# A sequence's group norm moved into the next sequence's first group, and its output projections one group later

## The chip, the cores and the metric

The kernel runs on one core of a Trainium2 chip. A core has TensorE (matmuls; PE in the profile, with PEld for its weight loads), VectorE (DVE), ScalarE (ACT), GpSimd (POOL) and SyncE (SP), whose queue issues most of the transfers. Each engine works through its own list of instructions in order and waits on semaphores for the others. Matmuls write to PSUM, which has eight banks here. The metric is the device time of the core in microseconds; lower is better.

## What is computed

x has 8 sequences of 512 tokens with 512 features. After a layer norm, the block computes a linear attention with decay in 16 heads, multiplies its output by a sigmoid gate, normalises each head's 32 features by their root mean square, and projects with Wo. Beside it stands a mixture of 16 experts (4 for each token) with a shared expert. The result is x + s * silu(ffn). Cut to what matters here:

```python
x = o * jax.nn.sigmoid(gate)
xg = x.reshape(b, n, HEADS, HEAD_DIM)
ms = jnp.mean(xg * xg, axis=-1, keepdims=True)
xg = xg * jax.lax.rsqrt(ms + EPS)
return xg.reshape(b, n, d) * weight      # then o @ Wo
# the block
x = L0_attn_x
xn = _layernorm(x, axis=-1)
s = _L0_attn_ref(xn, ...)
g = _silu(_L0_ffn_ref(xn, ...))
x = x + s * g
```

## The kernel before, in words

There are three stages. The first norms x, routes the tokens to experts and does the attention of sequences 0 and 1. The second runs the experts block by block. The third, which starts at about 740 us, does the attention of sequences 2 to 7 and, beside it, gathers the experts' results, adds them up and writes the output. Only the third is touched; `carry` is an empty list until it begins, so code under `if carry` belongs to it.

An attention sequence b works on the transposed activations xT: 4 groups g of 4 heads (128 features), 4 chunks of 128 tokens. In `sequence`, each group issues:

- `scores(b, g)` (L673): 12 small state matmuls (L684), then 16 score matmuls into four PSUM banks ps_0 to ps_3 (L695); a scan on VectorE gives the carried state, ScalarE copies it into a block matrix (L704), and VectorE multiplies the four banks by the decay mask into sc (L720).
- `step()`: a little work of the mixture of experts (`advance`, L1274): gathers and additions on GpSimd, two additions on VectorE (L1226, L1230), a Silu on ScalarE (L1233).
- for groups 0 and 1 the key and the query of two groups ahead (`rotated`, L637: a product of four matmuls, Silu on ScalarE, then shuffle, multiply by cos, multiply by sin and an addition on VectorE, L643 to L647); for groups 2 and 3 the value products of the next sequence (L587).
- `by_token` (L656): three transposes of the next group's keys.
- up to two deferred output projections of the sequence before (`project`, L785), by the table `fill`; `projected` is here `finish`, which multiplies the projection into the mixture's tile on VectorE (L1253), whereupon GpSimd adds x (L1257) and SP stores the tile.
- `output(b, g)`: the attention output (L731, L742), multiplied into the gate on VectorE (L746).

After the four groups comes the tail. With `defer`, as in the third stage, it issues the next sequence's gate (`gate_2`, L617, four Sigmoids) and last value product, and the norm of b itself: `squares` (L749: four Squares on ScalarE; 16 matmuls that sum them over each head into one bank, L756; a Sqrt, L760), `inverse` (a reciprocal on VectorE, L764), `normed` (L766: 16 matmuls that spread the factors over the features into four banks pb_0 to pb_3, L773; four multiplies on VectorE, L778). Between these stand the keys and queries of the next sequence's groups 0 and 1. `last_sequence` is the version for sequence 7, which has no next one; it projects sequence 6 from its own group 1 on.

What sets the order: within `on_pe()` and `behind(...)` a block is chained behind the last instruction of its engine; other instructions are put in order by a scheduler, and on each engine that order is then fixed. PSUM banks come from one pool by tag: four banks "a", two "d", one "k", one "m" (L105). An allocation of a tag takes the bank that was allocated longest ago, and the writer waits until that bank's readers are done. Key products and even value products take "m"; query products, odd value products, attention outputs and projections take "d"; scores (ps), gates (p2), the norm's sums (pr) and factors (pb) take "a".

Of the kernel before, what the change touches and what calls it, by code (L numbers as in the profile page):

```python
# [95 lines left out]
def tile_block(ctx: ExitStack, tc: tile.TileContext, a: dict, out: bass.AP):  # L96
# [8 lines left out]
    def bank(tag, name):  # L105
        return pp.tile([P, 512], F32, tag=tag, name=name, bufs={"a": 4, "k": 1, "m": 1, "d": 2}[tag])
# [474 lines left out]
    def value(b, t):  # L581
        if t == 0:
            v_of[b] = att.tile([P, NC, D], F32, tag="v", name=f"v_{b}", bufs=2)
        pv = bank("d" if t % 2 else "m", f"pv_{b}_{t}")
        for k in range(KC):
            with on_pe():
                nc.tensor.matmul(  # L587
                    pv, lhsT=xT_of[b][:, k, t * P : (t + 1) * P], rhs=wv[:, k, :],
                    start=(k == 0), stop=(k == KC - 1))
            between[0]()  # L590
        nc.scalar.copy(v_of[b][:, t, :], pv)
# [16 lines left out]
    def gate_2(b, tiles=range(NC)):  # L608
        if 0 in tiles:
            on_of[b] = home(b).tile([P, G, N], F32, tag="on", name=f"on_{b}", bufs=1)  # L610
        g1 = g1_of[b]
        p2s = {t: bank("a", f"p2_{b}_{t}") for t in tiles}
        with on_pe():
            for g in range(G):
                for t in tiles:
                    tq = slice(t * Q, (t + 1) * Q)
                    nc.tensor.matmul(  # L617
                        p2s[t][:, g * P : (g + 1) * P], lhsT=wg2[tq, g * P : (g + 1) * P],
                        rhs=g1[tq, :], start=True, stop=True)
        for t in tiles:  # L620
            nc.scalar.activation(
                on_of[b][:, :, t * P : (t + 1) * P],
                p2s[t].rearrange("p (g n) -> p g n", n=P), AF.Sigmoid)
        if NC - 1 in tiles:
            g1_of.pop(b)
# [27 lines left out]
    def query(b, g):  # L653
        qT_of[g] = rotated(b, g, "q", wq)
# [92 lines left out]


    def squares(b):  # L749
        pr = bank("a", f"pr_{b}")  # L750
        for g in range(G):
            sq = scr[0].tile([P, N], F32, tag="sc", name=f"sq_{b}_{g}", bufs=4)
            nc.scalar.activation(sq, on_of[b][:, g, :], AF.Square)
            with on_pe():
                for c in range(NC):
                    nc.tensor.matmul(  # L756
                        pr[c * Q : (c + 1) * Q, :C], lhsT=sel[:, H - HG - g * HG :][:, :Q],
                        rhs=sq[:, c * C : (c + 1) * C], start=(g == 0), stop=(g == G - 1))
        rs = att.tile([P, C], F32, tag="tmp", name=f"rs_{b}", bufs=TMP)
        nc.scalar.activation(rs, pr[:, :C], AF.Sqrt, bias=eps_rms, scale=1.0)  # L760
        rs_of[b] = rs

# [39 lines left out]
    def sequence(b, step, projected, before=None, defer=False, also=lambda: None):  # L802


        n = b + 1

        def project_tiles(q, ts):
            if q is not None:
                for t in ts:
                    projected(q, t, project(q, t))  # L810


        fill = ([0], [1], [2], [3], [], [], [], [])
        for g in range(G):
            scores(b, g)
            step()
            if g + 2 < G:
                key(b, g + 2)
            else:
                value(n, 2 * (g - 2))  # L820
            if g + 1 < G:
                by_token(b, g + 1)
            project_tiles(before, fill[2 * g])
            step()
            if g + 2 < G:
                query(b, g + 2)
                if g + 3 == G and n not in xT_of:
                    load_xT(n)
            if g + 2 == G:
                value(n, 1)  # L830
            if g == 0 and b not in on_of:
                gate_2(b)
            project_tiles(before, fill[2 * g + 1])
            if fill[2 * g + 1] == [NC - 1]:
                on_of.pop(before, None)
            output(b, g)
            if defer and g + 2 == G:
                gate_1(n)
            step()
        v_of.pop(b)  # L840
        if n == FIRST:
            gate_1(n)
            squares(b)
            inverse(b)
            value(n, 3)
            normed(b)
            return
        if defer:
            gate_2(n)
        value(n, 3)  # L850
        also()
        squares(b)
        step()
        inverse(b)
        key(n, 0)
        also()
        query(n, 0)
        normed(b)
        also()
        if not defer:  # L860
            step()
        key(n, 1)
        by_token(n, 0)
        if defer:
            step()
        query(n, 1)
        also()
        if not defer:
            gate_1(n)
            project_tiles(b, [0, 1])  # L870
            also()
            project_tiles(b, [2, 3])
            also()
            on_of.pop(b)
        step()

    def last_sequence(b, step, projected, before):


        pbs_of, sums = {}, []  # L880

        def squares_of(g):
            sq = scr[0].tile([P, N], F32, tag="sq", name=f"sq_{b}_{g}", bufs=2)
            nc.scalar.activation(sq, on_of[b][:, g, :], AF.Square)
            pr = bank("k" if g + 1 == G else "a", f"pr_{b}_{g}")
            with on_pe():
                for c in range(NC):
                    nc.tensor.matmul(
                        pr[c * Q : (c + 1) * Q, :C], lhsT=sel[:, H - HG - g * HG :][:, :Q],
                        rhs=sq[:, c * C : (c + 1) * C], start=True, stop=True)  # L890
            rs = att.tile([P, C], F32, tag="tmp", name=f"rs_{b}_{g}", bufs=TMP)
            nc.scalar.activation(rs, pr[:, :C], AF.Sqrt, bias=eps_rms, scale=1.0)
            nc.vector.reciprocal(rs, rs)
            rs_of[g] = rs

        def normed_of(g):
            rs = rs_of.pop(g)
            pbs = [bank(tag, f"pb_{b}_{g}_{c}")
                   for c, tag in enumerate("mddk" if g + 1 == G else "aaaa")]
            with on_pe():  # L900
                for c in range(NC):
                    cq = slice(c * Q, c * Q + H)
                    nc.tensor.matmul(
                        pbs[c][:, :C], lhsT=wge[cq, g * P : (g + 1) * P], rhs=rs[cq, :],
                        start=True, stop=True)
            for c in range(NC):
                oc = on_of[b][:, g, c * C : (c + 1) * C]
                nc.vector.tensor_tensor(oc, oc, pbs[c][:, :C], ALU.mult)

        def add_up(t, groups):  # L910
            if t == len(sums):
                sums.append(bank("a", f"pw_{b}_{t}"))
            with on_pe():
                for g in groups:
                    nc.tensor.matmul(  # L915
                        sums[t], lhsT=on_of[b][:, g, t * P : (t + 1) * P], rhs=wo[:, g, :],
                        start=(g == 0), stop=(g == G - 1))

        def project_before(t):
            projected(before, t, project(before, t))  # L920

        for g in range(G):
            scores(b, g)
            step()
            if g + 2 < G:
                key(b, g + 2)
            if g > 1:
                project_before(2 * g - 3)
            if g:
                squares_of(g - 1)  # L930
            if g + 1 < G:
                by_token(b, g + 1)
            step()
            if g + 2 < G:
                query(b, g + 2)
            if g in (1, 2):
                project_before(2 * g - 2)
                normed_of(g - 1)
            output(b, g)
            step()  # L940
        kept.clear()
        add_up(0, (0, 1))
        normed_of(G - 2)
        add_up(1, (0, 1))
        squares_of(G - 1)
        step()
        add_up(2, (0, 1))
        add_up(0, (2,))
        add_up(1, (2,))
        normed_of(G - 1)  # L950
        step()

        add_up(3, (0,))
        add_up(0, (3,))
        projected(b, 0, sums[0])
        add_up(3, (1,))
        add_up(1, (3,))
        projected(b, 1, sums[1])
        add_up(2, (2,))
        add_up(2, (3,))  # L960
        projected(b, 2, sums[2])
        add_up(3, (2, 3))
        projected(b, 3, sums[3])
        step()
# [399 lines left out]
```

## Time and profile before

| | |
|---|---|
| median of 3 runs | 1169.23 us (1165.0, 1169.23, 1175.48) |
| profiled execution | 1169.4 us, its span 1167.6 us, mean granted clock 0.996 |
| PE busy in the span | 1134.0 us (97%) |
| DVE, ACT, POOL busy | 705.6 us (60%), 460.2 us (39%), 452.2 us (39%) |
| 16 spreading matmuls (L773) of one norm | 1.17 us |
| 16 sum-of-squares matmuls (L756) of one norm | 1.08 us |
| product of four matmuls (L631, L785) | 3.60 us |
| score product (L720), one bank | 677 ns |

How to read it: a row of the timeline gives start, duration, engine, line, operation, what is written and read with the shapes, a count, and in brackets how long the engine stood idle before and what ended that. A line of the waits gives engine, line and tile, what was waited for, the total, the number of times and the longest. Matmuls are pipelined, so a row's duration runs some 0.1 us into the next row, and each matmul of the code shows as two there (a product of four as x8).

### The profile page before, as it was taken

Reading aid. Unit: us, or ns where it says so; the run is one execution under the profiler, and the core shown is the slowest. Engines: PE = TensorE matmul, PEld = TensorE weight load, DVE = VectorE, ACT = ScalarE, POOL = GpSimd, SP = SyncE. Lnnn points to the kernel's source line nnn. Section 1 sums busy time; section 2 is a strip of 40 time slices with the busy share of each in tenths; the row PEclk is TensorE's granted clock in tenths of the full one; section 3 lists DMA queues with packets and bytes.
Section 4 is the critical chain, followed back from the end, with each engine's and each line's share of the span. In section 5 each row is a group of like instructions: output and inputs, shape, how many; then the busy total and the mean of one; then the engine's idle time right before and its main releaser. Section 6 shows DMA issues by size and latency. Waiting matters only on the chain. (4 is left out here: it accounts for less than half of the span.)

```text
span 1167.6 us, 21692 instructions
## 1 busy us (share of the span) xinstructions
PE 1134.0 (97%) x7780; PEld 694.6 (59%) x7780; DVE 705.6 (60%) x1496; ACT 460.2 (39%) x1042; POOL 452.2 (39%) x432
## 2 busy tenths in 40 slices
PE   7999999989999999999999999999999999999997
PEld 3445554455577677777777775555554645545553
DVE  6358735996134344444444443968879598697784
ACT  3323324254364444444444442352252532523541
POOL 3213103200223333333333331782886858858211
PEclk9999999998999999999999999999999999999999
DMA  9975521290769989999999996951846637535012
GB/s 341 330 251 186 179 106 46 101 361 2 232 153 227 219 228 219 229 233 218 230 223 231 230 226 159 359 148 64 277 128 181 215 100 255 154 119 153 28 38 72
DMA packets 163787, 217.45 MB, mean 186 GB/s; under 512 B 89824, under 2 KB 99168, under 8 KB 161760
## 3 DMA queue, kind: packets, MB, share of 16 engines
q1 hardware_dynamic: 142272, 144.14, 41.9%
q0 software_dynamic: 21120, 70.34, 22.3%
q8 instruction: 65, 1.06, 0.4%
q10 hardware_dynamic: 288, 1.57, 0.4%
q14 instruction: 42, 0.34, 0.1%
HBM read 125.73 MB, written 72.43 MB: 170 GB/s over the span
## 5 line engine op out<-in xcount | busy, mean ns | idle before, releaser
L1112 PE MATMUL pgu<-wexp,xt 128*128 x1088 | 257.9, 380 | 2.7 <-ACT xt L1093 2.2
L1112 PEld LDWEIGHTS pgu<-wexp,xt 128*128 128x128 f32 x1088 | 205.8, 190 | 90.4 <-issue 29.5
L1071 POOL DMA_INDIRECT xg<-xn_d,slot x79 | 74.9, 948 | 243.0 <-DVE y L1142 156.4
L1095 ACT COPY xt<-pl 128x512 uint16<-128x512 uint16 x136 | 104.3, 767 | 142.9 <-DMA pl<-xg 75.9
L1117 DVE TENSOR_TENSOR slb<-slb,pgu 128x128 f32<-128x128 f32 x136 | 39.1, 288 | 196.6 <-ACT slb L1116 196.5
L1215 POOL DMA_INDIRECT yg<-y_d,place x128 | 142.4, 1112 | 31.4 <-issue 18.4
L1133 PE MATMUL py<-wexp,hT 128*128 x272 | 139.2, 594 | 0.0
L587 PE MATMUL pv<-wv,xT 128*128 128x512 f32 x256 | 122.2, 614 | 3.8 <-DMA xT<-xT_d 2.8
L631 PE MATMUL pk<-xT,wk 128*128 128x512 f32 x256 | 118.3, 603 | 0.0
L631 PE MATMUL pq<-xT,wq 128*128 128x512 f32 x256 | 115.9, 593 | 0.3 <-PEq L1177 0.3
L785 PE MATMUL pw<-wo,on 128*128 128x512 f32 x224 | 100.6, 596 | 5.5 <-DVE m L1253 4.9
L1071 POOL DMA_INDIRECT more<-xn_d,slot x57 | 53.8, 944 | 108.3 <-DVE y L1142 107.4
L1257 POOL TENSOR_TENSOR xo<-xo,m 128x512 f32<-128x512 f32 x31 | 45.3, 1461 | 128.4 <-DVE m L1253 121.2
L720 DVE TENSOR_TENSOR sc<-ps,dmask 128x512 f32<-128x512 f32 x128 | 79.1, 677 | 0.9 <-PE ps L695 0.8
L631 PEld LDWEIGHTS pq<-xT,wq 128*128 128x128 f32 x256 | 47.2, 191 | 52.8 <-issue 51.3
L587 PEld LDWEIGHTS pv<-wv,xT 128*128 128x128 f32 x256 | 46.6, 195 | 50.3 <-issue 42.8
L631 PEld LDWEIGHTS pk<-xT,wk 128*128 128x128 f32 x256 | 46.2, 190 | 50.0 <-issue 47.6
L1142 DVE TENSOR_SCALAR y<-py,xg 128x512 f32<-128x512 f32 x79 | 59.2, 750 | 27.4 <-PE py L1133 27.2
L785 PEld LDWEIGHTS pw<-wo,on 128*128 128x128 f32 x224 | 41.2, 190 | 54.9 <-issue 45.4
L1116 ACT ACTIVATE slb<-pgu 128x128 f32<-128x128 f32 x136 | 37.8, 278 | 80.0 <-PE pgu L1112 79.7
L704 ACT COPY blocked<-state 32x96 f32<-32x96 f32 x96 | 30.6, 319 | 79.0 <-DVE state L699 78.1
L1142 DVE TENSOR_SCALAR y<-py,more 128x512 f32<-128x512 f32 x57 | 42.7, 750 | 20.0 <-PE py L1133 20.0
(173 smaller groups left out, 1729.9 us busy)
## 6 DMA issues: line engine op xcount, KB each, us to landing
y_d<-y SPq DMA_DIRECT2D x136, 256.0 KB, 2.9
wexp<-in_experts SPq DMA_DIRECT2D x14, 768.0 KB, 7.8
sh_d<-sh SPq DMA_DIRECT2D x32, 256.0 KB, 3.1
m<-sh_d SPq DMA_DIRECT2D x32, 256.0 KB, 4.4
xo<-in_x SPq DMA_DIRECT2D x32, 256.0 KB, 3.8
out<-xo SPq DMA_DIRECT2D x31, 256.0 KB, 2.0
x<-in_x SPq DMA_DIRECT2D x7, 1024.0 KB, 7.6
xT_d<-xT SPq DMA_DIRECT2D x7, 1024.0 KB, 6.5
```

Of the source, the lines that this page charges most:

```text
L587: nc.tensor.matmul(pv, lhsT=xT_of[b][:, k, t * P : (t + 1) * P], rhs=wv[:, k, :], start=(k == 0), stop=(k == KC - 1))
L631: nc.tensor.matmul(ps, lhsT=w[:, k, g * P : (g + 1) * P], rhs=xT_of[b][:, k, :], start=(k == 0), stop=(k == KC - 1))
L720: nc.vector.tensor_tensor(s, pss[j].rearrange("p (c t) -> p c t", t=C), dmask[:, g * HG + j].unsqueeze(1).to_broadcast([P, NC, C]), ALU.mult)
L785: nc.tensor.matmul(pw, lhsT=on_of[b][:, g, t * P : (t + 1) * P], rhs=wo[:, g, :], start=(g == 0), stop=(g == G - 1))
L1071: nc.gpsimd.indirect_dma_start(out=row(i), out_offset=None, in_=xn_d, in_offset=bass.IndirectOffsetOnAxis(ap=slot[:, i : i + 1], axis=0))
L1095: nc.scalar.copy(xt[:, KP:, :].bitcast(U16).rearrange("p k (t h) -> p h k t", h=2), turned(i).rearrange("p (h k) t -> p h k t", h=2))
L1112: nc.tensor.matmul(pg[:, : 2 * F], lhsT=xt[:, k, :], rhs=wflat[:, bass.ds(off + k * 2 * F, 2 * F)], start=(k == 0), stop=(k == KC - 1))
L1117: nc.vector.tensor_tensor(sl, sl, pg[:, F : 2 * F], ALU.mult)
L1133: nc.tensor.matmul(py, lhsT=hT_of.pop(i), rhs=wflat[:, bass.ds(off_of.pop(i) + KC * 2 * F, D)], start=True, stop=True)
L1142: gone.append(nc.vector.tensor_scalar(y, py, row(i).bitcast(F32)[:, bass.ds(at, 1)], None, ALU.mult).ins)
L1215: nc.gpsimd.indirect_dma_start(out=yg, out_offset=None, in_=y_d, in_offset=bass.IndirectOffsetOnAxis(ap=place[:, r, g : g + 1], axis=0))
L1257: nc.gpsimd.tensor_tensor(xo, xo, m, ALU.add)
```

## The change

The norm of a sequence in the third stage leaves the tail and is issued in the next sequence's group 0: the squares and their sums ahead of the scores, the reciprocal behind them, the spreading and the multiplies behind the query of group 2 and ahead of the attention output. The deferred projections, which need it, move from groups 0 and 1 to groups 1 and 2. The sums take a bank of tag "d" and not "a", and their square roots a tile of their own. In sequence 7, `last_sequence` takes the norm of sequence 6 in the same places; its projections stay. Sequences 0 and 1 keep their order.

```diff
@@ -747,7 +747,7 @@
 
 
     def squares(b):
-        pr = bank("a", f"pr_{b}")
+        pr = bank("d" if carry else "a", f"pr_{b}")
         for g in range(G):
             sq = scr[0].tile([P, N], F32, tag="sc", name=f"sq_{b}_{g}", bufs=4)
             nc.scalar.activation(sq, on_of[b][:, g, :], AF.Square)
@@ -756,7 +756,8 @@
                     nc.tensor.matmul(
                         pr[c * Q : (c + 1) * Q, :C], lhsT=sel[:, H - HG - g * HG :][:, :Q],
                         rhs=sq[:, c * C : (c + 1) * C], start=(g == 0), stop=(g == G - 1))
-        rs = att.tile([P, C], F32, tag="tmp", name=f"rs_{b}", bufs=TMP)
+        rs = scr[0].tile([P, C], F32, tag="rs", name=f"rs_{b}") if carry else att.tile(
+            [P, C], F32, tag="tmp", name=f"rs_{b}", bufs=TMP)
         nc.scalar.activation(rs, pr[:, :C], AF.Sqrt, bias=eps_rms, scale=1.0)
         rs_of[b] = rs
 
@@ -810,9 +811,13 @@
                     projected(q, t, project(q, t))
 
 
-        fill = ([0], [1], [2], [3], [], [], [], [])
+        fill = ([], [], [0], [1], [2], [3], [], [])
         for g in range(G):
+            if g == 0 and before is not None:
+                squares(before)
             scores(b, g)
+            if g == 0 and before is not None:
+                inverse(before)
             step()
             if g + 2 < G:
                 key(b, g + 2)
@@ -830,6 +835,8 @@
                 value(n, 1)
             if g == 0 and b not in on_of:
                 gate_2(b)
+            if g == 0 and before is not None:
+                normed(before)
             project_tiles(before, fill[2 * g + 1])
             if fill[2 * g + 1] == [NC - 1]:
                 on_of.pop(before, None)
@@ -847,6 +854,16 @@
             return
         if defer:
             gate_2(n)
+            value(n, 3)
+            step()
+            key(n, 0)
+            query(n, 0)
+            key(n, 1)
+            by_token(n, 0)
+            step()
+            query(n, 1)
+            step()
+            return
         value(n, 3)
         also()
         squares(b)
@@ -857,21 +874,17 @@
         query(n, 0)
         normed(b)
         also()
-        if not defer:
-            step()
+        step()
         key(n, 1)
         by_token(n, 0)
-        if defer:
-            step()
         query(n, 1)
         also()
-        if not defer:
-            gate_1(n)
-            project_tiles(b, [0, 1])
-            also()
-            project_tiles(b, [2, 3])
-            also()
-            on_of.pop(b)
+        gate_1(n)
+        project_tiles(b, [0, 1])
+        also()
+        project_tiles(b, [2, 3])
+        also()
+        on_of.pop(b)
         step()
 
     def last_sequence(b, step, projected, before):
@@ -920,7 +933,11 @@
             projected(before, t, project(before, t))
 
         for g in range(G):
+            if g == 0:
+                squares(before)
             scores(b, g)
+            if g == 0:
+                inverse(before)
             step()
             if g + 2 < G:
                 key(b, g + 2)
@@ -933,6 +950,8 @@
             step()
             if g + 2 < G:
                 query(b, g + 2)
+            if g == 0:
+                normed(before)
             if g in (1, 2):
                 project_before(2 * g - 2)
                 normed_of(g - 1)
```

## The prediction

> **What bounds the kernel now.** I read the split of the span by stage first, then TensorE's list of waits in the last stage, then the timelines of TensorE and VectorE around the place that is edited, and last the granted clock. Only the last stage is touched, so the first rows are the five sequences of it that matter, cut where each reaches the value product of its third group (columns: window and length, then busy us of PE, PEld, DVE, ACT, POOL with instruction counts, granted clock, DMA share, GB/s).
>
> ```profile
> 758.98:832.97 73.99, 73.99 (x646) 40.57 (x645) 58.41 (x94) 28.34 (x63) 44.97 (x38) 1.00 0.46 145
> 832.97:908.79 75.82, 74.53 (x646) 40.41 (x645) 66.11 (x96) 28.66 (x64) 58.81 (x48) 1.00 0.60 181
> 908.79:985.38 76.59, 74.47 (x645) 40.41 (x645) 60.07 (x95) 28.70 (x64) 56.40 (x48) 1.00 0.56 172
> 985.38:1063.06 77.68, 75.55 (x645) 41.36 (x645) 60.78 (x93) 28.81 (x64) 57.11 (x48) 1.00 0.52 158
> ```
>
> The matmul work is the same in the four windows, and in the first TensorE never stops: 73.99 us is the price of a sequence without a stall. The others lose 1.83, 2.60 and 3.69 us, 8.1 in all. That is all the stage can give back by better order, 0.7% of the kernel. TensorE's waits say where most of it is lost:
>
> ```profile
> PE pw L785 <- DVE m L1253: 4.9, 4, 1.9
> ```
>
> The second deferred projection waits for a bank of tag d that VectorE has not emptied. VectorE is behind in the first two groups of a sequence and idle later. Now the place of the edit, sequence 3 (start, duration, instruction):
>
> ```profile
> 797.34 1.17 PE L695 MATMUL ps<-qT,kT 32*128 32x128 f32 x32
> 798.44 3.70 PE L631 MATMUL pk<-xT,wk 128*128 128x512 f32 x8
> 801.98 0.49 PE L663 MATMUL pk<-ident,kT 128*128 128x128 f32 x3
> ...
> 805.74 3.60 PE L631 MATMUL pq<-xT,wq 128*128 128x512 f32 x8
> 809.17 3.60 PE L785 MATMUL pw<-wo,on 128*128 128x512 f32 x8
> 812.61 0.83 PE L731 MATMUL po<-qd,blocked 128*128 128x128 f32 x6
> ...
> 814.57 1.17 PE L695 MATMUL ps<-qT,kT 32*128 32x128 f32 x32
> ```
>
> ```profile
> 783.55 0.95 DVE L764 RECIPROCAL rs<-rs 128x128 f32<-128x128 f32 x1 [5.68 <-ACT rs L760]
> ...
> 791.85 2.48 DVE L778 TENSOR_TENSOR on<-on,pb 128x512 f32<-128x512 f32 x4
> ...
> 801.33 2.48 DVE L720 TENSOR_TENSOR sc<-ps,dmask 128x512 f32<-128x512 f32 x4
> ...
> 810.07 0.72 DVE L643 STREAM_SHUFFLE swq<-sq 128x512 f32<-128x512 f32 x1
> ```
>
> The reader is to see that VectorE begins the masked score products (801.33) 2.9 us after the scores are done (798.44), and that TensorE does not mind: two projections (pw) lie between those scores and the next ones.
>
> **The change part by part.** It moves 16 sum-of-squares matmuls (1.01 us), 16 spreading matmuls (1.10), four Square (2.19 on ScalarE) and a Sqrt, a reciprocal (0.95) and four norm multiplies (2.48) from the tail of a sequence into the next one's group 0, five times, and four projections (3.43 us each) a group later. TensorE's work is unchanged. The instruction order of the two kernels shows that it does so: in the tail no norm is left; pr stands behind pq_1 and ahead of the first scores, pb between pq_2 and po_0, pw_0 and pw_1 in group 1, pw_2 and pw_3 in group 2.
>
> Sums of squares: the four Squares keep their early place on ScalarE, so pr finds its operands; 0. The bank of tag d is freed by the Sqrt long before pq_2 needs it two products later; 0. On DVE the reciprocal now stands in front of the four score products: 0.95 each time, counted below.
>
> Projections: their multiplies (0.6 each) and GpSimd's additions leave group 0 for groups 1 and 2, where pv products give VectorE time. SP's queue has the same transfers; the xo loads go later, and the xT load, issued at 827.8 for a use at 908.8, has 80 us to spare. 0.
>
> The spread is the costly part. Its four pb banks are of tag a, of which there are four, and the next four allocations of that tag are the score banks of group 1. So ps_1 now waits for the four norm multiplies. In VectorE's new order these stand behind the rotation of query 2. A floor follows: pq_2 ends at T; ScalarE's Silu and the handover take 0.73 (809.34 to 810.07); shuffle, cos and sin 1.93; four multiplies and the last addition of the rotation five slots of 0.60: 5.7. TensorE meanwhile has pb 1.10, po 1.66, states 0.30: 3.1. The last score bank opens at 5.7, and some 0.8 of the 1.10 of scores is left then, so scores end at 6.5 in place of 4.2: at least 2.3 us lost per sequence, 12 in five.
>
> If VectorE is behind, it is more. Let L be how late the score products of group 0 start behind their scores, and m the expert-mixture operations that stand before the norm multiplies. VectorE then needs 2.40 + 2.54 (key rotation) + 1.93 + 3.0 = 9.9 us after that start; TensorE reaches the end of ps_1 after 3.54 + 0.33 + 3.43 + 1.10 + 1.66 + 0.30 + 1.10 = 11.5. The wait is L + m + 9.9 + 0.8 - 11.5 = L + m - 0.8. Before, L is 2.9, 4.6, 5.3, 8.0 (against scores without their own wait) and 2.7 us in sequences 3 to 7. The norm's leaving takes 2.4 off, the reciprocal adds 0.95; scores come 1.1 earlier, the tail's rotations about 1.0: 1.35 less where VectorE is never idle (5 and 6; in 4 a multiply by s moves ahead and leaves about 4.3), unchanged in 3 and 7, where it waits for the next Silu instead. With m of 1.3, 1.3, 1.9, 1.3 and 0.6 from the new order (0.6 to 0.7 each), the waits are 3.4, 4.8, 5.1, 7.1 and 2.5: 23 us. That this bank pair can hold TensorE is in the trace: in sequence 6 the scores, 1.17 elsewhere, took 2.69, behind the norm multiplies (1022.74 to 1025.13).
>
> ```profile
> 1023.73 2.69 PE L695 MATMUL ps<-qT,kT 32*128 32x128 f32 x32
> ```
>
> Against it, the 8.1 us of old losses go: pw_0 and pw_1 come after a pause in which VectorE has caught up (from the last norm multiply to the multiply by pw_0 it has 9 to 11 us of work, TensorE 11.5 before pw_1). I take 2 us off for GpSimd's additions to xo, which left group 0: beside them VectorE's two-input operations took 1.1 to 2.1 in place of 0.68. Net 23 - 8 - 2 = +13.
>
> **The clock.** Rows of stage two, where TensorE stopped for 2.77 and for 0.79 us:
>
> ```profile
> 262.00:264.00 2.00, 0.42 (x1) 0.42 (x2) 2.00 (x5) 0.00 (x0) 0.00 (x0) 0.83 0.06 25
> 264.00:266.00 2.00, 2.00 (x3) 0.75 (x3) 2.00 (x4) 0.28 (x1) 0.00 (x0) 0.50 0.00 0
> ...
> 284.00:286.00 2.00, 2.00 (x6) 0.78 (x5) 1.93 (x3) 0.00 (x0) 0.00 (x0) 0.50 0.00 0
> ```
>
> After both, the clock was 0.50 for some 3.4 us, about 1.6 us of lost work each. The Trainium skill, "TensorE: Matmul & The Clock Gate", section "Why this matters for your kernels", tells to leave no idle gap over about 3 us between matmul bursts, since an idle window halves the clock. By that rule three waits (sequences 4 to 6) drop it, +4.8; by the second row, where 0.79 us amid small matmuls was enough, all five, +8, for pb, po, states and scores are small matmuls too. But gaps of 1.1 to 1.9 us between long matmuls in the last stage left it at 1.00. I take the rule: +5.
>
> ScalarE gets one more table load in each group 0 (Sqrt now stands between Silus, 10 loads for 5): 1.28 us by its row, and the next operation starts as it ends (857.91, then 859.20). "ScalarE: Activation LUTs", section "What ACT_TABLE_LOAD costs", adds 1.38 us of drain per switch. By the row the Silu of key 2 ends as VectorE comes to it in sequences 3 and 7, 0; by the page those two would be 1.4 later, +2.8. The row decides, 0.
>
> **Sum.** The profiled execution took 1169.4 us (span 1167.6), the median of the runs is 1169.23, so they are one. 1169.4 + 13 + 5 = 1187.
>
> **Rivals.** (1) VectorE keeps up and every wait is at its floor, with the clock held: 12 - 8.1 = +4, 1173. For it: VectorE is busy 58 to 66 of 76 us. Against: L never falls under 2.7 in five sequences. (2) Faster: the backlog that stops pw is what counts, and moved to group 1 it vanishes, while the new wait is hidden: -8.1, 1161. It needs the norm multiplies to be done within 3.1 us of pq_2's end, which the order of the rotation ahead of them (2.66 with Silu) allows for one bank of four. Its ceiling is 0.7%, so it is no win of over 1%. (3) The clock falls in all five and pw_1 waits again as before (4.9): 1187 + 3 + 5 = 1195, more if GpSimd's additions meet the rotations.
>
> **How the numbers follow.** Runs spread from 1165 to 1175, so 1% (11.7 us) is about what can be told from no change. Forecast 0.62, its own range 1180 to 1192; floor 0.20; faster 0.08; worse 0.10. Holding 8 in 10: 1172 to 1197. Over 1180.9: most of the forecast and the worst case, 0.70; faster by over 1% 0.03; the rest 0.27.
>
> **What would show it.** Right: scores of group 1 at 3 to 8 us in place of 1.17 in each of sequences 3 to 7, waiting for the norm multiplies; the wait of pw for m gone or under 2 us; the clock at 0.5 after some of these pauses; a tail without holes; periods of 77 to 81 us. Wrong: scores at 1.2 to 2, or the pause in front of pr or of pw. The size is wrong if VectorE's lag at the first products is far from 3 to 7 us.

## The result, and the profile after

The changed kernel takes 1205.86 us (median of 4 runs, 1202.78 to 1213.91) against 1172.36 of the kernel before, run beside it: ratio 1.0294, 95% interval 1.0258 to 1.033, slower. The profiled execution took 1202.78 us with a span of 1201.0, which is 33.4 more than the span of before, and its mean granted clock is 0.981 (0.996 before). The direction was forecast, and so was the wait that causes it, but 1187 was 19 us short and the range ended at 1197.

The place of the loss is the one that was named. TensorE's list of waits in the last stage of the changed kernel (what waits, for what; us in total, times, longest):

```profile
PE ps L695 <- DVE on L779: 22.8, 7, 7.9
PE pb L916 <- DVE on L921: 0.4, 1, 0.4
PE pk L663 <- DVE state L699: 0.3, 1, 0.3
```

The 4.9 us of pw are gone, and the scores of group 1 now wait for the norm multiplies (L779 in the changed file). The windows from the value product of one third group to the next, for sequences 3 to 6 (columns as in the prediction):

```profile
829.33:914.05 84.72, 78.60 (x648) 43.84 (x644) 63.63 (x95) 30.14 (x65) 57.28 (x49) 0.94 0.55 172
914.05:999.94 85.89, 78.01 (x648) 43.82 (x645) 61.05 (x94) 29.94 (x65) 55.45 (x47) 0.94 0.47 150
999.94:1085.39 85.45, 78.91 (x648) 44.05 (x645) 58.86 (x93) 29.85 (x65) 58.27 (x49) 0.94 0.47 141
```

They were 75.82, 76.59 and 77.68: 26.0 us of the 33.4 are here, and the granted clock fell from 1.00 to 0.94. TensorE is idle for 6 to 8 us in each, and its busy time rose by 3 to 4 us though it does the same work. Sequence 5 shows both. First TensorE (start, duration, instruction, idle time before it):

```profile
957.71 1.17 PE L695 MATMUL ps<-qT,kT 32*128 32x128 f32 x32
958.82 3.70 PE L631 MATMUL pk<-xT,wk 128*128 128x512 f32 x8
...
962.68 3.60 PE L631 MATMUL pq<-xT,wq 128*128 128x512 f32 x8
966.21 1.32 PE L774 MATMUL pb<-rs,wge 16*128 16x128 f32 x32
...
969.22 0.37 PE L684 MATMUL pk<-v,kd 128*32 128x32 f32 x24
977.47 3.86 PE L695 MATMUL ps<-qT,kT 32*128 32x128 f32 x32 [7.88 <-DVE on L779]
981.26 5.15 PE L631 MATMUL pk<-xT,wk 128*128 128x512 f32 x8
```

The scores of group 0 end at 958.82, and the next ones could start at 969.6. They start 7.88 later and then take 3.86 where the first ones took 1.17, and the key product behind them takes 5.15 where the one of group 0 took 3.70. VectorE in that stretch:

```profile
963.91 2.41 DVE L720 TENSOR_TENSOR sc<-ps,dmask 128x512 f32<-128x512 f32 x4
966.24 0.98 DVE L1245 SCALAR_TENSOR_TENSOR m<-m,sg,yg 128x512 f32<-128x512 f32 x1
...
967.77 2.15 DVE L645 TENSOR_TENSOR kT<-sk,cos 128x512 f32<-128x512 f32 x1
969.84 0.68 DVE L646 TENSOR_TENSOR swk<-swk,sin 128x512 f32<-128x512 f32 x1
...
973.00 1.13 DVE L645 TENSOR_TENSOR qT<-sq,cos 128x512 f32<-128x512 f32 x1
974.05 0.68 DVE L646 TENSOR_TENSOR swq<-swq,sin 128x512 f32<-128x512 f32 x1
974.76 2.05 DVE L647 TENSOR_TENSOR qT<-qT,swq 128x512 f32<-128x512 f32 x1
976.74 1.87 DVE L779 TENSOR_TENSOR on<-on,pb 128x512 f32<-128x512 f32 x3
```

L, the lag of the first score product, is 963.91 - 958.82 = 5.1. VectorE is never idle. What the sum did not have are the 2.15, 1.13 and 2.05: the same instructions take 0.68 otherwise. GpSimd adds two SBUF tiles at those moments:

```profile
968.08 1.27 POOL L1243 TENSOR_TENSOR yg<-yg,yg 128x512 f32<-128x512 f32 x1
...
971.93 1.65 POOL L1276 TENSOR_TENSOR xo<-xo,m 128x512 f32<-128x512 f32 x1 [1.17 <-DVE m L1272]
...
974.98 1.27 POOL L1240 TENSOR_TENSOR yg<-yg,yg 128x512 f32<-128x512 f32 x1
```

The granted clock (last but two of the columns) just after the pauses of sequences 3 to 7:

```profile
810.00:812.00 2.00, 2.00 (x15) 1.26 (x10) 2.00 (x4) 0.57 (x2) 1.40 (x1) 0.53 0.12 8
892.00:894.00 2.00, 2.00 (x24) 1.79 (x27) 2.00 (x5) 0.00 (x0) 0.00 (x0) 0.50 0.47 131
978.00:980.00 2.00, 2.00 (x18) 1.73 (x20) 2.00 (x5) 0.00 (x0) 1.84 (x2) 0.50 0.48 151
1064.00:1066.00 2.00, 2.00 (x24) 1.80 (x27) 2.00 (x5) 0.33 (x2) 1.45 (x2) 0.50 0.45 127
1146.00:1148.00 2.00, 2.00 (x3) 0.68 (x2) 1.12 (x2) 0.00 (x0) 0.00 (x0) 0.50 0.00 0
```

It fell in all five, also after the idle time of 0.90 us in sequence 7 and after these two in sequence 3:

```profile
806.98 0.48 PE L695 MATMUL ps<-qT,kT 32*128 32x128 f32 x2 [1.13 <-DVE on L779]
808.18 2.60 PE L695 MATMUL ps<-qT,kT 32*128 32x128 f32 x30 [0.71 <-DVE on L779]
```

### The profile page after: what moved, and what is told of

It reads as the page before. It is cut to its first block, busy times and chain, and to the rows that moved or that the text cites. A ratio compares the mean times of both kernels' runs of the same rounds, so it can differ in the third digit from the quotient of the medians.

```text
span 1201.0 us, 21675 instructions
## 1 busy us (share of the span) xinstructions
PE 1151.5 (96%) x7780; PEld 708.0 (59%) x7780; DVE 702.6 (59%) x1496; ACT 466.8 (39%) x1047; POOL 450.0 (37%) x432
## 5 line engine op out<-in xcount | busy, mean ns | idle before, releaser
L1234 POOL DMA_INDIRECT yg<-y_d,place x128 | 138.9, 1085 | 31.2 <-issue 19.4
L631 PE MATMUL pk<-xT,wk 128*128 128x512 f32 x256 | 125.2, 633 | 0.0
L631 PEld LDWEIGHTS pk<-xT,wk 128*128 128x128 f32 x256 | 50.2, 203 | 58.4 <-issue 55.8
L695 PE MATMUL ps<-qT,kT 32*128 32x128 f32 x1024 | 52.1, 301 | 24.2 <-DVE on L779 22.8
L695 PEld LDWEIGHTS ps<-qT,kT 32*128 32x128 f32 x1024 | 43.1, 199 | 28.4 <-DVE on L779 25.4
```

Of the source, the lines that this page charges most:

```text
L631: nc.tensor.matmul(ps, lhsT=w[:, k, g * P : (g + 1) * P], rhs=xT_of[b][:, k, :], start=(k == 0), stop=(k == KC - 1))
L695: nc.tensor.matmul(pss[j][:, cs], lhsT=kT[hs, cs], rhs=qT[hs, cs], start=True, stop=True)
L1234: nc.gpsimd.indirect_dma_start(out=yg, out_offset=None, in_=y_d, in_offset=bass.IndirectOffsetOnAxis(ap=place[:, r, g : g + 1], axis=0))
```

## The experiments

Eighteen runs in five sets; the runs of one set share a chip and its runs of the kernel before. That kernel took 1171.1 us in the first set and 1170.7 in the fourth, and 1181.6, 1184.2 and 1181.7 in the second, third and fifth. In these three the traces show idle times of TensorE, between small matmuls, to which the profile gives no releaser ("issue"). The chip alone does not decide it: the record gives the first three sets the same chip number, although an expectation below speaks of another chip. So ratios are compared, and small differences only within one set.

**The changed kernel again** (fourth set).

> The changed kernel as it is, beside the other runs on one chip. Theory A: pauses are set by VectorE, not by the chip's gaps, so the ratio to before stays at 1.025 to 1.034. If it depends on the chip: outside of that.

1209.2 us, ratio 1.031 (1.0283 to 1.0337), the waits of the scores 22.6 us in all. The result stands.

**The norm multiplies ahead of the rotation** (first set). The query product is issued, then the norm, then the rotation, whose first instruction is queued behind the last multiply (cut; `last_sequence` gets the same):

```diff
-                query(b, g + 2)
+                if g == 0 and before is not None:
+                    pq = product(b, 2, "q", wq, "d")
+                    normed(before)
+                    qT_of[2] = rotated(b, 2, "q", wq, pq, lambda: behind(DVE))
+                else:
+                    query(b, g + 2)
```

> The changed kernel with one thing moved: on VectorE the four norm multiplies stand ahead of the rotation of query 2 instead of behind it; TensorE's order is untouched. Theory A (the scores of group 1 wait for the tag-a banks that the multiplies empty): the four instructions of that rotation (2.5 to 3 us, more where GpSimd's additions meet them) leave the path in each of the five sequences, so the waits of those scores fall from 36 us to 18 to 23, and the time from 1203 to about 1185 to 1190. Rival B (VectorE is simply out of time in the first two groups and TensorE pays the same amount at the next place whatever the order): the pause moves to the scores or the output of group 1 or to the key product, its sum stays near 36, the time stays at 1200 to 1206. Rival C (the deferral of the projections or the table loads cost it): no change of the time.

1188.86 us, ratio 1.0147 (1.011 to 1.0184). Its waits in the last stage:

```profile
PE ps L696 <- DVE on L780: 14.2, 3, 5.2
PE pk L664 <- DVE state L700: 1.4, 3, 0.8
```

One multiplication by cos stayed ahead of the multiplies, three instructions of the rotation moved behind. The pause did not turn up elsewhere and the time is where theory A had it: rival B falls, and the place on VectorE is worth about half of the loss. In sequences 3 and 7 the idle time is gone and the scores take 2.64 and 1.97; the other three pauses are 4.2, 5.2 and 4.8.

**The deferral alone** (first set). The kernel before with one line of the change:

```diff
-        fill = ([0], [1], [2], [3], [], [], [], [])
+        fill = ([], [], [0], [1], [2], [3], [], [])
```

> The kernel before with one part of the change alone: the deferred projections a group later (groups 1 and 2 instead of 0 and 1); the norm stays in the tail of its own sequence, the last sequence is as before. Theory A: the deferral is harmless and takes away the wait of the projections for the expert mixture (4.9 us in the trace of before) and leaves a small wait of the scores of group 1 where VectorE lags, since the two projections no longer lie between them and the scores of group 0 (3.6 + 0.5 + 3.6 us of products and 2 us of output still do): 1162 to 1170. Rival C (the deferral is the cost): 1180 or more, with the scores of group 1 waiting for the score products of group 0 by several us.

1186.49 us, ratio 1.0118 (1.0088 to 1.0148). The expectation missed: the deferral is not harmless. The scores of group 1 pass, but behind them a key product ends and the transposes for group 2 need bank k, which the scan of the states must have read:

```profile
PE pk L663 <- DVE state L699: 14.5, 4, 6.3
```

```profile
963.83 1.17 PE L695 MATMUL ps<-qT,kT 32*128 32x128 f32 x32
964.93 3.70 PE L631 MATMUL pk<-xT,wk 128*128 128x512 f32 x8
974.89 0.48 PE L663 MATMUL pk<-ident,kT 128*128 128x128 f32 x1 [6.26 <-DVE state L699]
```

The second fence is TensorE's timeline in sequence 5 of this run: key product, then 6.26 us of nothing. So rival C has the time right but not the place. The two projections that stood in group 0 (6.9 us) are longer than this wait; they were the work under which VectorE caught up, as the next run shows.

**Filling group 0 again** (second set). The changed kernel, with two value products of the next sequence in group 0 instead of group 2 (their x is loaded a sequence earlier; in group 2 a projection stands ahead of the transposes):

```diff
+            if g == 0 and before is not None:
+                value(n, 0, "d")
...
                 normed(before)
+                value(n, 1, "m")
```

> The changed kernel, with the first two value products of the next sequence in its group 0, where the two projections used to stand (the first ahead of query 2, the second between the spread and the output), the norm and the projections as in the change. Theory A (the pause is there because group 0 lost the 7.1 us of TensorE work that lay over VectorE's backlog, and the bank wait shows it): the pauses of 1.8 to 7.9 us shrink to 0 to 3, the clock falls in two or three sequences at most, 1166 to 1177. Rival B (VectorE's work bounds the sequence, or the norm multiplies behind the rotation stop TensorE whatever lies ahead): pauses of 4 us or more remain, 1188 or more.

1184.59 us, ratio 1.0028 (1.0001 to 1.0055); by the ratio about 1174 in the terms of the first set, inside theory A's band. Of waits for VectorE its list in the last stage has one of the scores for the multiplies, one for the scan (0.6) and the 0.4 of pb in the last sequence, besides some 6 us of "issue":

```profile
PE pk L684 <- issue: 3.0, 5, 1.2
...
PE ps L695 <- DVE on L779: 0.9, 1, 0.9
```

The norm is where the change puts it, the multiplies still stand behind the rotation and use the same banks, and nine tenths of the loss are gone (0.3% against 2.9%). The early value products by themselves do not explain it: in the kernel before, in the last experiment below, they bring 0.0 to 0.5%. So the bank wait is how the lost cover shows, and not a price that the new place must pay.

**The squares back in the tail** (second and fourth set). `squares(b)` and `inverse(b)` return to the tail of the sequence, `normed` stays in group 0.

> The changed kernel with one part undone: squares, their sum, the Sqrt and the reciprocal stand in the tail of their own sequence as before; spread and norm multiplies stay in the next one's group 0. Theory A (that part costs little: 0.95 us of VectorE ahead of the score products in the sequences where it is behind, one table load that nobody waits for): 3 to 6 us less, 1199 to 1203. Rival (the Sqrt between the Silus of group 0 makes ScalarE late and is a good part of the loss): 1193 or less.

1217.67 us, ratio 1.032 (1.0285 to 1.0354), no gain, so both answers of the expectation missed; since no changed kernel ran beside it, once more:

> The changed kernel with squares, Sqrt and reciprocal in the tail, beside the changed kernel. In its first run the waits of the scores summed to 22.1 us against 22.8 in the changed kernel, so the part costs nothing that shows: within 4 us of the changed kernel. The first expectation (3 to 6 us less) would need the reciprocal's 0.95 us on the path.

1203.87 us, ratio 1.0283 (1.0255 to 1.0311), against 1.031 of the changed kernel beside it. By the medians that is 5.3 us less, a little more than the 4 that were allowed for; the intervals overlap, and the scores wait 22.5 us against 22.6. That part adds nothing to the waits; whether it costs some 5 us of time or none is not shown.

**GpSimd's additions on one column** (first set; the rest of the additions is left out). `ys[0]`, `ys[2]` and `xo` are added with `[:, :1]` on every operand.

> The changed kernel in which GpSimd's three additions of a mixture tile cover one column of 512 only (that part of the mixture and of the residual is left out), so that they no longer run beside VectorE's operations. Theory A with contention as the term that was mis-sized: cos, sin and mixture operations of VectorE between the first score product and the norm multiplies go from 1.1-2.2 us back to 0.6-0.7, the pauses of sequences 4, 5 and 6 fall from 9-10.6 us to 5-7, the sum from 36 to 22-26, the time to 1186 to 1192. If contention is not it: the pauses stay within 2 us of what they are, and the time within 1199 to 1206.

1185.97 us, ratio 1.011 (1.0072 to 1.0147). VectorE in sequence 5 of this run, to be held against the fence of the changed kernel above:

```profile
960.14 2.42 DVE L720 TENSOR_TENSOR sc<-ps,dmask 128x512 f32<-128x512 f32 x4
962.48 0.74 DVE L1245 SCALAR_TENSOR_TENSOR m<-m,sg,yg 128x512 f32<-128x512 f32 x1
...
963.76 0.68 DVE L645 TENSOR_TENSOR kT<-sk,cos 128x512 f32<-128x512 f32 x1
...
967.53 0.72 DVE L645 TENSOR_TENSOR qT<-sq,cos 128x512 f32<-128x512 f32 x1
...
968.94 0.69 DVE L647 TENSOR_TENSOR qT<-qT,swq 128x512 f32<-128x512 f32 x1
969.55 2.47 DVE L779 TENSOR_TENSOR on<-on,pb 128x512 f32<-128x512 f32 x4
```

From the first score product to the first norm multiply it is 9.41 us here, and 12.83 with full additions. The waits of the scores fall from 22.8 to 8.8 us. Contention, that is VectorE's rows of 1.1 to 2.2 us beside GpSimd's additions, is in the pause.

Whether the kernel before pays for it as well needed a control, the same edit in the kernel before (second set):

> The control of the run with small additions: the kernel before, with GpSimd's three additions of a mixture tile on one column of 512 only (that part is left out). The changed kernel gained about 20 us by it (1205.9 to 1186.0). Theory A (contention matters where VectorE holds TensorE up, and before it hardly did): before gains only out of its 8.1 us of losses, 1163 to 1169, so that most of the 20 us belong to the change. If the additions cost both kernels alike: before falls to about 1151, which is below what its own TensorE work allows, so this would show that the additions slow something else too.

1242.05 us, ratio 1.0528 (1.0491 to 1.0564): it fell outside of both answers. The waits for VectorE are gone from TensorE's list but for 0.8 us, and others stand in it. From this list, then a stretch of its timeline with GpSimd's:

```profile
PE ps L695 <- issue: 8.8, 34, 0.6
PE pk L684 <- issue: 7.1, 14, 1.2
PE pg L601 <- issue: 6.3, 13, 1.0
```

```profile
955.41 0.97 POOL L1215 DMA_INDIRECT yg<-y_d,place  x1 [0.15 <-issue]
956.04 1.09 PE L601 MATMUL pg<-xT,wg 128*32 128x128 f32 x4 [1.00 <-issue]
...
956.68 0.95 POOL L1215 DMA_INDIRECT yg<-y_d,place  x1 [0.30 <-issue]
...
957.47 0.62 PE L601 MATMUL pg<-xT,wg 128*32 128x128 f32 x3 [0.34 <-issue]
```

Strings of small matmuls come in threes and fours, with up to 1 us between, while the gathers, no longer spaced by additions, follow each other at once. I ran the changed kernel's version and the control side by side (third set), and the control once more (fifth):

> The changed kernel with the additions on one column, once more, beside its control on one chip: in the control's first run TensorE stood still for some 30 us in strings of small matmuls with nothing to wait for in the profile ("issue"), while GpSimd issued its gathers back to back. If this belongs to the small additions themselves, this kernel shows such gaps now too, and 1210 or more. If it belongs to that chip or run, it repeats its 1.011 of the time of before, 1183 to 1188.

> The kernel before with the additions on one column, again. If the gaps were the chip's or the run's: the control that was wanted, 1163 to 1169 if contention costs before little, so that most of the 20 us that the changed kernel gains are the change's own; about 1151 if it costs both alike. If the gaps belong to this kernel: 1230 or more again, and the control tells nothing on contention.

> The kernel before with the additions on one column, a third time. On a chip without TensorE's unexplained gaps: if the additions cost the kernel before what stalls it has, 1161 to 1166 (its 8 us of losses are the most that it can gain); if the contention hits the changed kernel alone, 1168 to 1172. On a chip with them: 1230 to 1280, and this stays open.

They took 1276.03 (ratio 1.0757, 1.0703 to 1.081), 1250.98 (1.0563, 1.0515 to 1.0612) and 1244.71 us (1.0521, 1.0467 to 1.0574). The same program that took 1186 us in the first set takes 1276 in the third. Its gathers follow each other as closely in the first set, about half of them within 1.45 us of the one before in both (a fifth in the changed kernel), and there it has no such gap: so the gathers alone do not make the gaps. In the sets in which gaps occur at all, they are larger with the small additions, 25 to 36 us in all in place of 5 to 6. The clock adds to them: in the first of these runs of the kernel before, the matmuls of the last stage take 457.0 us in place of 411.1, at a clock of 0.94 there. These runs tell nothing on contention in the kernel before.

**One addition twice** (fourth set). This keeps the gathers apart: the second addition of a tile is also made into a spare tile, in the changed kernel and in the kernel before (cut).

```diff
+            nc.gpsimd.tensor_tensor(twice, ys[2], ys[3], ALU.add)
             nc.gpsimd.tensor_tensor(ys[2], ys[2], ys[3], ALU.add)
```

> The changed kernel with the second addition of every mixture tile made once more into a spare tile (1.27 us of GpSimd each, six tiles a sequence, 7.6 us). Theory A (contention lengthens the pause, in the changed kernel some 3 us in each of sequences 4 to 6 for three additions a tile): 4 to 10 us slower than the changed kernel, and at least 3 us more than the same edit costs the kernel before. If contention is not in the pause: both within 3 us of their own kernel.

> The kernel before with the same addition twice. Theory A (VectorE has slack under the projections of group 0): 0 to 4 us slower than before. If contention costs both kernels alike: as many us as it costs the changed one.

The changed kernel took 1216.47 us (ratio 1.0386, 1.0364 to 1.0409), 7.3 more than beside it without the edit. The kernel before took 1193.16 (1.0182, 1.0158 to 1.0205), 22.5 more, outside of both of its answers: its projections wait 8.7 us for the mixture, its sums of squares 5.8 for ScalarE's gate and its transposes 5.8 for the scan. The second half of the changed kernel's expectation is wrong. But the edit does two things to the kernel before. VectorE's busy time in the last stage rises from 326.2 us (trace of before) to 348.4, since its rows beside GpSimd's additions get longer; and VectorE also stands idle for GpSimd's sums, which now come later:

```profile
DVE m L1233 <- POOL yg L1227: 20.3, 8, 4.8
DVE m L1229 <- POOL yg L1221: 19.8, 8, 4.1
```

These two are 6.8 and 4.1 us in the trace of before, and 7.6 and 5.2 in the changed kernel with the edit. So the run shows that the kernel before pays for more work on GpSimd, and not how much of that is contention. That the changed kernel pays less because much of it falls into a pause that is there anyway is a guess.

**What the clock costs.** Unused matmuls of 128x512 between the output of group 0 and the scores of group 1 (first set: 5, 8 and 6 in sequences 4 to 6):

> The changed kernel with 5, 8 and 6 unused matmuls of 128x512 (4.6, 7.4 and 5.5 us) added in sequences 4, 5 and 6 between the output of group 0 and the scores of group 1, where TensorE pauses. Theory A: VectorE sets the end of the pause, so the added work is free; what the clock cost comes back: the scores of group 1 at 1.2 us instead of 3.9 and the key product at 3.7 instead of 5.0 to 5.7 in these three, about 8 us in all, 1194 to 1197. If the clock costs nothing beyond what the pauses cover: 1201 to 1204. If TensorE, not VectorE, sets that stage (the pause is only waiting that is made up elsewhere): 1215 or more.

1201.84 us, ratio 1.0242 (1.0202 to 1.0283): 17.1 us of added TensorE work cost nothing, so VectorE sets the pause. The time is the one named for a clock that costs nothing by itself. But idle times of 0.2 to 1.6 us were left in front of and among the scores, and the clock in the windows there was 0.70, 0.87 and 0.91. So the pause was closed (third set: 3, 8, 9, 7 and 2 matmuls in sequences 3 to 7):

> The changed kernel with unused matmuls (3, 8, 9, 7 and 2 of 128x512 in sequences 3 to 7, 2.8 to 8.2 us) that close the whole pause ahead of the scores of group 1. The earlier filler left 0.65 to 1.6 us open, and the scores still took 3.1 to 3.6 us, so it didn't tell what the clock costs. Theory A (after a pause the half clock stretches the scores by 1.8 to 2.7 us and the key product behind them by 1.3 to 2.0): with no pause both run at full clock (1.2 and 3.7 us) in all five, 13 to 18 us less than the changed kernel, 1188 to 1193. If the half clock costs nothing of its own (VectorE would hold TensorE up at the next place anyway): 1202 to 1207. If the first bank still opens later than the filler ends in some: in between, with those scores at over 3 us.

1201.38 us, ratio 1.0125 (1.0073 to 1.0177) in a set where before takes 1184. Sequence 5, and the clock there and in sequence 6:

```profile
981.45 7.99 PE L848 MATMUL spare<-xT,wk 128*128 128x512 f32 x18
989.37 0.40 PE L684 MATMUL pk<-v,kd 128*32 128x32 f32 x24
989.69 2.85 PE L695 MATMUL ps<-qT,kT 32*128 32x128 f32 x32
992.47 3.70 PE L631 MATMUL pk<-xT,wk 128*128 128x512 f32 x8
```

```profile
989.00:993.00 4.00, 3.76 (x59) 2.42 (x58) 4.00 (x8) 0.00 (x0) 3.03 (x3) 1.00 0.49 143
1073.00:1077.00 4.00, 3.77 (x59) 2.69 (x59) 4.00 (x8) 0.94 (x3) 2.34 (x3) 1.00 0.51 151
```

The key product is back at 3.70 (5.15 in the changed kernel), the clock at 1.00. From the scores of group 0 to those of group 2, sequences 3 to 6 take 32.2, 38.0, 38.9 and 38.1 us, against 34.1, 40.0, 41.1 and 40.7: the clock costs about 2.2 us a sequence, by estimate 11 in five. The ratio fell by more than these 11 us are worth; since the sets differ, I rest on the trace.

**A kernel that beats both?** The same idea without the change's norm: the kernel before, with three value products in the projections' places of groups 0 and 1 and the projections behind them (second, third and fifth set; cut).

```diff
+            if early and g < 2:
+                values((2 * g, "d"))
...
+            if early and g == 0:
+                values((1, "m"))
+            elif early:
+                projects(*([(0, "d")], [(2, "d")], [(3, "m")])[g - 1])
```

> The kernel before, with three value products of the next sequence in the places of the projections in groups 0 and 1, and the projections in groups 1 to 3 in their places (the next but one x is loaded a sequence earlier for it); the norm stays in the tail. Theory A (what counts is TensorE work in group 0 that does not wait for VectorE; the banks of a value product are emptied by ScalarE): the wait of the projections for the mixture (4.9 us) goes and no other comes, 1162 to 1167. Rival (the place of the projections itself matters, as in the run that only deferred them, 1186): 1175 or more, with the transposes of group 2 waiting for the scan of the states.

> The kernel before with value products of the next sequence in groups 0 and 1 and the projections behind them, again on another chip, since in its first run 6 us of TensorE gaps with nothing to wait for stood in the profile. Theory A: the wait of the projections (4.9 us) is gone and no other comes, ratio to before 0.991 to 0.997. If the first gain was chance: 0.999 to 1.003.

> The kernel before with value products of the next sequence in groups 0 and 1 and the projections behind them, a third time. Theory A: 0.992 to 0.998 of before on a chip without the gaps, with no wait of the projections for the mixture left.

1177.13, 1181.05 and 1180.18 us; ratios 0.9954 (0.9927 to 0.9981), 0.9986 (0.9949 to 1.0023) and 0.9996 (0.9966 to 1.0026). The wait of the projections for the mixture is gone in all three traces, 1.6 to 1.7 us of waiting for the scan came in its place, and in time there is no difference that can be relied on. It beats the changed kernel, not the one before.

## Why the prediction was right and wrong

**The wait that replaces another: right.** The old wait of pw is gone, the new one is where it was put, behind the banks of tag a. L was forecast at 2.9, 4.3, 4.0, 6.6 and 2.7 and is 3.0, 4.5, 5.1, 6.5 and 2.7. The floor alone (rival 1) and the hidden wait (rival 2) are out.

**The size: the step that failed is the 9.9 in "L + m + 9.9 + 0.8 - 11.5", VectorE's chain with every operation at its undisturbed duration, and its companion, "I take 2 us off for GpSimd's additions".** Count from the end of the scores of group 0 to the start of the key product behind the scores of group 1, less the 11.66 us that this way takes without a wait (by the rows of sequence 3): the five delays are 3.8, 9.1, 10.8, 10.5 and 2.8 us, 36.9 in all. Of these, 3.0 belong to the clock: at full clock, in the run that closed the pause, the key product starts 1.2 us after the last norm multiply ends, here up to 2.1. That leaves 33.9 for a forecast of 23. Of the 11 in between, 9.0 are VectorE's stretched operations between the first score product and the last multiply (3.1, 3.6 and 2.3 us over their usual durations in sequences 4 to 6), which the small additions removed: 9.41 us of chain in place of 12.83 in sequence 5. L adds 1.3. From the last multiply to the key product it is 1.2 where the sum had 0.8, another 2.1 in five; its other terms were 1.4 too high. The 2 us that were to come off did not: the trace of before had shown rows of 1.1 to 2.1 us, and the sum treated them as an accident of group 0 that would leave with the xo additions. There were still three additions to a tile, and VectorE was now awaited.

**The clock: +5 was about +11, the other step that failed.** The prediction set a rule of the Trainium skill ("TensorE: Matmul & The Clock Gate", "Why this matters for your kernels": no idle gap over about 3 us between bursts) against its own row of 0.79 us amid small matmuls, and took the rule. The row was right: five drops, two of them after idle times of 0.7 to 1.1 us, and in the first filler run after 0.65 and 0.69. The key products behind the scores took 5.0 to 5.7 us in place of 3.7: 1.4, 2.0, 1.5, 1.3 and 1.7 more, 7.9 in all. With the 3.0 on the scores that is 10.9, and the run that closed the pauses gave 2.2 a sequence.

**The sum made again:** 33.9 + 10.9 - 8.1 = 36.7, for the 33.4 between the two spans; the last stage began 1.6 us earlier in the profiled execution of after, and 1.7 are not resolved. Rival 3 had the five drops, but not its cause for the rest: pw does not wait again.

**The parts costed at nothing.** Squares, Sqrt and reciprocal: right for the waits; some 5 us of time are left open. The table load: its row was right, the next operation starts as the load ends (957.29 + 1.28, then 958.58), and no drain is seen. The projections: wrong as it stands. Their multiplies do leave group 0, as the text said, but their matmuls leave it too, and that alone costs 15 us of before's time. The formula for the wait did count TensorE's way without them, so the number was in the sum; what was missed is that it is the deferral which opens the gap, whether the norm moves or not: without the norm the wait of the scan stands there, with it the wait of the scores.

**What stays open:** how much contention costs the kernel before, what decides whether an idle time drops the clock, and why the times of one program differ by 90 us between sets.

## What to carry to other kernels

Before moving matmul work out of a stretch, ask which engine is behind there: the work may be the cover under which it catches up, and then the wait comes at the next buffer that the two share. When one engine becomes the one that is waited for, sum its chain with the durations that the trace shows in that stretch beside the other engines, not with the undisturbed ones. And put a price on the clock for every new pause amid small matmuls, also for one of 0.7 us: here it was 1.7 to 2.9 us each.

## What the hardware showed that was not expected

The clock fell to 0.50 after idle times of 0.7 to 1.1 us amid small matmuls, and in these five pauses it stayed at 1.00 in the run that closed them. The length of the idle time does not decide it alone: in the kernel before, 1.13 to 1.91 us ahead of a projection left it at 1.00, and with one addition twice, 1.89 us at the same place dropped it to 0.50 (that projection took 5.40 us in place of 3.60). A second GpSimd addition (1.27 us a tile) cost the kernel before 22.5 us, while VectorE's busy time rose by 22 us and its waits for GpSimd's sums by 29; which of the two cost how much is not shown. And TensorE can stand still in strings of small matmuls, up to 1.8 us at a time and 25 to 36 us in all, with no releaser in the profile: 1186 us in one set of runs and 1276 in another, for the same program on the same chip number. GpSimd's gathers follow each other closely in both, so they are not enough to cause it; what does is open.
